# Layer 3 in column tiles, Toeplitz tiles held ahead of it, and DMAs moved between queues in a four-layer convolution kernel

## The chip, the cores and the metric

The kernel runs on one core of one Trainium2 chip. The metric is the device time of one execution in microseconds (us). A core has TensorE for matmuls (PE in the profile; its weight loads are shown apart as PEld), VectorE (DVE), ScalarE (ACT), GpSimd (POOL) and SyncE (SP). SP, ACT and POOL also issue DMAs, each in the order of its own instruction stream: an issue that has to wait holds up what stands behind it on that engine.

## The reference, cut to what matters

Four layers follow each other on `x` of shape (4, 32, 32, 16): batch, two image axes, channels.

```
_gn: group norm over 8 groups of 2 channels

# layers 0, 1, 2, each with its own M, Wp, G
inputs  = _gn(x)
first   = einsum('ijpq,bpqc->bijc', M2, inputs)
shifted = conv3x3(inputs, K(G))                 # one 3x3 filter bank for every (i, j)
diff    = relu(inputs[:, :, :, None, None, :] - shifted)
second  = einsum('ijpq,bpqijc->bijc', W2, diff)
x = x + first - second

# layer 3
inputs = _gn(x)
a, b = pad(denumerator), pad(numerators[0])
h    = irfft2(rfft2(b, (32, 32)) / rfft2(a, (32, 32)))     # a 32 x 32 filter per channel pair
y    = linear 2-D convolution of inputs with h, plus h0 at lag 0, cut to 32 x 32
x = x + y
```

## The kernel before, in words

**Layers 0 to 2.** The output positions (i, j) are worked through in 128 blks of eight positions (128 columns: eight positions of 16 filters). For one blk and one batch, called a tile here, TensorE computes the convolution as three accumulated matmuls on each half of the image (L336): `ga` and `gb` hold taps of G in float32, `gn` holds the rest, split in a high and a low part. The operands `im` are eight shifted copies of the normalised image (`im..0`, `im..1`) and four copies of its parts for the last tap (`im..2`), each of 16 channels by two halves. A half is 64 of the 128 rows, so the two halves are separate row tiles of the array. VectorE then takes the minimum with zero, multiplies with W and sums, in one pass over the two PSUM banks (L344). Four such pairs of banks exist (`ps`, bufs=4).

One W tile serves two blks; six are kept. G comes in chunks of eight blks (GC = 8): `load_g` issues five DMAs on SP, `prepare_g` subtracts on POOL (L266), casts on ACT (L270) and corrects on VectorE (L273). Two chunks of `ga`, `gb` and `gn` are kept, and one of `g9`.

**Jobs.** `conv_layer` runs the first and the last chunk of a layer in two jobs each, batches 0 and 1, then 2 and 3, so that one pair of batches can be normalised while the other is still worked on. Each of the fourteen jobs between covers a chunk with all four batches. `k` is the blk within its job. After each tile `step()` advances the pending image generators by one; after each blk of the fourteen jobs `beside` is advanced by one: first `first_term` (the M product, ending with `fd`, `xf` and `xr`), then, in layer 0, `impulse_response` (the filter of layer 3), and in layer 2 the Toeplitz loads. Program order decides the order on each engine; a `yield` is a place where the rest is put off to the next call.

**Images.** `make_image` normalises two batches (`group_norm`: sums over rows on VectorE, over groups by a matmul with `avg`), writes the image and its edges to DRAM (`img<-y` on SP, `img<-e` on ACT), and reads the shifted copies back with 24 DMAs (L166), in turn on SP and ACT. The first image of layer 0 stands alone at the start; the second is made during the first job.

**Completion semaphores.** The DMAs issued by SP and ACT share eight completion semaphores in turn, so that an issue waits until the DMA eight places ahead of it in the program has landed. POOL's DMAs have eight of their own.

**Layer 3.** The filter, written to DRAM as `hd`, is read as eight Toeplitz tiles `t` of four lags each (TQ = 4), eight DMAs a tile, three tiles at a time. For each of 32 lags `dq` and four chunks `cc`, one matmul (L564) with all 128 rows and 128 columns adds `y3`, shifted by the lag, times the filter into one bank `po`. Output position rows below the lag get zeros: `y3` is padded with 31 of them.

Where layer 3 and the W loads stand in the code:

```
lhsT=y3[:, cc, 31 - dq : 31 - dq + S, :]      # 128 columns: 32 rows of the image by 4 batches
rhs=t[:, :, q * PITCH : q * PITCH + S - 8 * cc]  # 512, 384, 256, 128 columns for cc = 0..3
...
load_g(0, 0)                                  # start: G, then one W tile, then the first image
load_w()
...
for _ in range(3):                            # after the first image: three W tiles
    load_w()
```

Of the kernel before, what the change touches and what calls it, by code (L numbers as in the profile page):

```python
# [48 lines left out]
HLEN = 8 + S * PITCH  # L49
TQ = 4  # L50


@with_exitstack
def conv_stack_kernel(ctx, tc, x, M, W, G, den, num, h0, cst, dft, one, idp, idq, out):
# [18 lines left out]
    def small_psum():  # L73
        return pair_psum()[:, 0, :]
# [20 lines left out]
    td = dram.tile([NK, 2, S, 2 * P], F32, name="td")  # L95

    def group_norm(xt):

# [3 lines left out]
        yield  # L102
        pm = small_psum()
        nc.tensor.matmul(pm[:, :2], lhsT=avg, rhs=s, start=True, stop=True)  # L104
        mean = small.tile([P, 2], F32, tag="mean", name="mean")
        nc.vector.tensor_copy(mean, pm[:, :2])
        xc = work.tile([P, 2, NBLK], F32, tag="xc", name="xc")
# [8 lines left out]
        yield  # L116
        pv = small_psum()
        nc.tensor.matmul(pv[:, :2], lhsT=avg, rhs=ss, start=True, stop=True)
        v = small.tile([P, 2], F32, tag="v", name="v")
        nc.vector.tensor_scalar(v, pv[:, :2], 1e-5, None, ALU.add)  # L120

# [13 lines left out]
    def make_image(a, xt):  # L135
# [24 lines left out]
        ]  # L160
        jobs = [(n // 4, n % 4, 0, TAPS[n]) for n in range(8)]
        jobs += [(2, n, 1 + n % 2, 8) for n in range(4)]
        for k, slot, which, tap in jobs:
            for half, q in enumerate((nc.sync, nc.scalar)):
                at, p = 64 * half + C * slot, 4 * half + tap // 3
                q.dma_start(  # L166
                    out=ims[a][k][at : at + C]
                    .bitcast(F32)
                    .rearrange("c l b cc x -> c l (b cc x)")[:, :, :RUN],
                    in_=img[a][which, p : p + 4, :, tap % 3 : tap % 3 + RUN].rearrange(  # L170
                        "l c x -> c l x"
                    ),
                )

# [5 lines left out]
    def first_term(layer, xt):  # L180
# [38 lines left out]
        for h in range(2):  # L219
            for b in range(B):  # L220
                for cc in range(2):
                    at = 64 * h + C * b
                    nc.scalar.dma_start(out=fv[h, cc, b], in_=ft[at : at + C, cc])  # L223
            yield
        xf = work.tile([P, B, NBLK], F32, tag="xf", name="xf")
        nc.scalar.dma_start(
            out=xf.rearrange("p b n -> p (b n)"), in_=fd.rearrange("p b h cc q -> p (b h cc q)")
# [10 lines left out]

    def load_g(layer, ch):
        layer, ch = at = chunk(layer, ch)  # L240
        if layer == 3 or at in gr:
            return
        ga = gs.tile([P, GC, P], F32, tag="ga", name="ga")
        gb = gs.tile([P, GC, P], F32, tag="gb", name="gb")
        g9 = gp.tile([P, GC, P], F32, tag="g9", name="g9")
        src = G[layer][:, bass.ts(ch, GC * P)]
        for half in range(2):
            rows = slice(64 * half, 64 * half + 64)
            nc.sync.dma_start(out=ga[rows].rearrange("r n m -> r (n m)"), in_=src[:64])
            nc.sync.dma_start(out=gb[rows].rearrange("r n m -> r (n m)"), in_=src[64:P])  # L250
        nc.sync.dma_start(
            out=g9.rearrange("r n m -> r (n m)"),
            in_=src[P : P + C].unsqueeze(0).to_broadcast([8, C, GC * P]),
        )
        gr[at] = ga, gb, g9
# [21 lines left out]

    def load_w():

        layer, at = divmod(len(wts), NBLK // 2)  # L280
        if layer == 3:
# [3 lines left out]
        src = W[layer][cc, :, q : q + 2, :].rearrange("p k m -> p (k m)")  # L285
        nc.sync.dma_start(
            out=wt.rearrange("p k m -> p (k m)"),
            in_=src.unsqueeze(1).to_broadcast([8, C, 2 * S * S]),
        )
        wts.append(wt)  # L290

    todo = []
# [8 lines left out]
    def conv_layer(layer, xt, finish, side=()):  # L301
# [14 lines left out]
        for job, (blks, batches) in enumerate(jobs):  # L316
            pairs = job < 2, job >= len(jobs) - 2
            for k, blk in enumerate(blks):
                if any(pairs):

                    if k in ((4, 6) if job != len(jobs) - 2 else (0, 2)):
                        load_w()
                elif k % 2 == 0:
                    load_w()
                if job:
                    if k == 1:
                        load_g(layer, blk // GC + 1)
                    if k == 6:
                        prepare_g(layer, blk // GC + 1)
                wt = wts[64 * layer + blk // 2][:, blk % 2, :]  # L330
# [34 lines left out]
    def impulse_response():  # L365
# [81 lines left out]
        with tc.tile_pool(name="fs2", bufs=1) as fs:  # L447
# [10 lines left out]
            for u in range(4):  # L458
                g = 32 * u
                nc.scalar.dma_start(out=v[g : g + 1], in_=rows[u, 0:1])  # L460
                nc.scalar.dma_start(out=v[g + 1 : g + 2], in_=rows[u, 32:33])
                nc.scalar.dma_start(out=v[g + 2 : g + 32], in_=rows[u, 2:32])
            yield
            yield
            yield
            for part in range(4):
# [15 lines left out]
            nc.gpsimd.tensor_tensor(hs[:, :, :, 0], hs[:, :, :, 0], h0s, ALU.add)  # L482
            nc.scalar.dma_start(
                out=hd[:, :8].rearrange("(n m) r -> n m r", m=4), in_=hs[:, 0, :4, S:]
            )
            for h in range(2):
                for l in range(2):
                    n = 64 * (2 * h + l)
                    nc.scalar.dma_start(
                        out=hd[n : n + 64, 8:].rearrange("m (q r) -> q m r", r=PITCH),  # L490
# [4 lines left out]
    def load_toeplitz(k):  # L495

        t = tp.tile([P, C, TQ * PITCH], F32, tag="t", name="t")
        hv = hd.rearrange("(j i) t -> i j t", j=C)
        for p in range(8):
            at = 8 + k * TQ * PITCH - p  # L500
            (nc.sync, nc.scalar)[p % 2].dma_start(
                out=t[p * C : (p + 1) * C], in_=hv[:, :, at : at + TQ * PITCH]
            )
        return t

    load_g(0, 0)
    load_w()
    images = [make_image(a, xs) for a in range(2)]
# [4 lines left out]
    drain()  # L513
    for _ in range(3):
        load_w()
    todo.append(images[1])
# [16 lines left out]

    tp = ctx.enter_context(tc.tile_pool(name="tp", bufs=3))
    ts = []

    def toeplitz():
        for k in range(3):
            ts.append(load_toeplitz(k))
            yield  # L540

    xs = conv_layer(2, xs, norm3, toeplitz())
    drain()

    xr = work.tile([P, 4, S, B], F32, tag="xf", name="xr")
    nc.scalar.copy(xr, xs.rearrange("p b (cc q) -> p cc q b", q=S))
# [7 lines left out]

    po = small_psum()
    pov = po.rearrange("n (j r) -> n j r", j=C)
    for k in range(S // TQ):
        if k and k + 2 < S // TQ:
            ts.append(load_toeplitz(k + 2))
        t = ts[k]  # L560
        for q in range(TQ):
            dq = k * TQ + q
            for cc in range(4):
                nc.tensor.matmul(  # L564
                    pov[:, :, 8 * cc :],
                    lhsT=y3[:, cc, 31 - dq : 31 - dq + S, :].rearrange("p q b -> p (q b)"),
                    rhs=t[:, :, q * PITCH : q * PITCH + S - 8 * cc],
                    start=(dq == 0 and cc == 0),
                    stop=(dq == S - 1 and cc == 3),
                )  # L570
    nc.vector.tensor_tensor(xo, xo, pov.rearrange("n j r -> n r j"), ALU.add)  # L571
    nc.sync.dma_start(out=out, in_=xo)
# [83 lines left out]
```

## Time and profile before

| | us |
|---|---|
| Time, median of 3 runs | 3216.81 (3214.71 to 3222.22) |
| The profiled execution: its time | 3216.64 |
| The profiled execution: span from first to last instruction | 3214.8 |
| Mean granted TensorE clock | 0.994 |

| engine | busy us | share of the span |
|---|---|---|
| PE | 3148.2 | 98% |
| PEld | 1678.7 | 52% |
| DVE | 2054.8 | 64% |
| ACT | 75.7 | 2% |
| POOL | 171.9 | 5% |

How to read it. The chain of waits follows the work that ended last back from the end: each piece has its start, its length and what it was, so a DMA in it is one that somebody waited for. The timeline lists instructions in order of time; a bracket at the end of a line holds how long the engine was idle before it and who released it. Groups of instructions have count, busy time, mean duration in ns and the idle time before them. Time by stretches gives the busy time of each engine between two moments, then the granted clock, the busy share of the 16 DMA engines (overlapping packets can take it above 1) and GB/s. A float32 matmul appears as two records, and so does its weight load. Names are written without the buffer numbers: `img<-y` is the DMA that writes the image to DRAM, `w<-in_W_dram` a W tile.

### The profile page before, as it was taken

Reading aid. Unit: us, or ns where it says so; the run is one execution under the profiler, and the core shown is the slowest. Engines: PE = TensorE matmul, PEld = TensorE weight load, DVE = VectorE, ACT = ScalarE, POOL = GpSimd, SP = SyncE. Lnnn points to the kernel's source line nnn. Section 1 sums busy time; section 2 is a strip of 40 time slices with the busy share of each in tenths; the row PEclk is TensorE's granted clock in tenths of the full one; section 3 lists DMA queues with packets and bytes.
Section 4 is the critical chain, followed back from the end, with each engine's and each line's share of the span. In section 5 each row is a group of like instructions: output and inputs, shape, how many; then the busy total and the mean of one; then the engine's idle time right before and its main releaser. Section 6 shows DMA issues by size and latency. Waiting matters only on the chain.

```text
span 3214.8 us, 38408 instructions
## 1 busy us (share of the span) xinstructions
PE 3148.2 (98%) x15852; PEld 1678.7 (52%) x15852; DVE 2054.8 (64%) x3294; ACT 75.7 (2%) x98; POOL 171.9 (5%) x124
## 2 busy tenths in 40 slices
PE   6999999999999999999999999999989999999998
PEld 3545566666666544444544445454444444444445
DVE  4666765666666766666666666766656666666660
ACT  0000000000000000000000000000000000000000
POOL 0002310000000000000000000000000000000000
PEclk9999999999999999999999999999999999999999
DMA  6544344343333554333433343365473343333306
GB/s 148 156 115 116 88 109 94 86 103 88 88 98 90 107 154 118 99 89 88 99 96 86 86 105 87 80 143 144 99 127 89 98 99 89 87 99 92 86 1 85
DMA packets 106383, 322.18 MB, mean 100 GB/s; under 512 B 29214, under 2 KB 59360, under 8 KB 81632
## 3 DMA queue, kind: packets, MB, share of 16 engines
q1 hardware_dynamic: 68608, 302.69, 39.2%
q10 hardware_dynamic: 37600, 17.04, 3.4%
q8 instruction: 124, 2.03, 0.3%
q14 instruction: 51, 0.42, 0.1%
HBM read 313.01 MB, written 6.68 MB: 99 GB/s over the span
## 4 chain that ended last, share of the span: by engine, by line
PE 94%; DMA 4%; DVE 1%; ACTq 0%; issue 0%; SPq 0%; POOL 0%; ACT 0%; DVEq 0%; POOLq 0%
PE pt L336 90%; PE pt L564 2%; DMA t<-hd 1%; DMA img<-y 1%; DMA im<-img 1%; PE pt L199 1%; DMA td<-s 1%; DMA v<-td 0%; DMA fd<-ft 0%; DVE junk L344 0%; DMA h0s<-in_h_dram 0%; PE pt L470 0%; ACTq L223 0%; PE pt L387 0%; POOL hs L452 0%
## 5 line engine op out<-in xcount | busy, mean ns | idle before, releaser
L344 DVE SCALAR_TENSOR_TENSOR junk<-pt,w 128x1024 f32<-128x1024 f32 x1536 | 1880.8, 1224 | 1031.7 <-PE pt L336 1017.4
L336 PE MATMUL pt<-im,ga 64*128 64x512 f32 x6144 | 1834.4, 592 | 38.0 <-DMA im<-img 20.5
L336 PE MATMUL pt<-im,gb 64*128 64x512 f32 x6144 | 1824.4, 589 | 0.9 <-DMA im<-img 0.9
L336 PE MATMUL pt<-im,gn 64*128 64x512 f32 x3072 | 1487.7, 807 | 1.9 <-DMA im<-img 1.9
L336 PEld LDWEIGHTS pt<-im,gb 64*128 64x128 f32 x6144 | 706.5, 186 | 737.7 <-issue 705.0
L336 PEld LDWEIGHTS pt<-im,ga 64*128 64x128 f32 x6144 | 708.6, 188 | 422.8 <-DVE junk L344 246.6
L336 PEld LDWEIGHTS pt<-im,gn 64*128 64x128 f32 x3072 | 355.3, 186 | 295.4 <-issue 290.2
L266 POOL TENSOR_TENSOR ga<-ga,cs 128x1024 f32<-128x1024 f32 x48 | 113.4, 2362 | 2215.5 <-DMA ga<-in_G_dram 2153.5
L273 DVE TENSOR_TENSOR gn<-g,gn 32x1024 fp32r<-32x1024 f32 x96 | 118.0, 1229 | 34.3 <-ACT gn L270 32.3
L344 DVE DVE_READ_ACCUMULATOR junk<-pt,w 128x1 f32 x1536 | 127.3, 83 | 0.0
L270 ACT CAST gn<-g 128x1024 fp32r<-128x1024 f32 x48 | 50.2, 1047 | 2318.7 <-DMA g<-in_G_dram 2020.4
L564 PE MATMUL pt<-t,y 128*128 128x512 f32 (+3 forms) x256 | 70.4, 438 | 0.0
L564 PEld LDWEIGHTS pt<-t,y 128*128 128x128 f32 x256 | 44.2, 193 | 26.2 <-issue 16.2
L571 DVE TENSOR_TENSOR xo<-xo,pt 128x512 f32<-128x512 f32 x1 | 0.7, 689 | 70.8 <-PE pt L564 70.8
L199 PE MATMUL pt<-mt,yt 128*64 128x512 f32 x96 | 21.9, 598 | 0.0
L231 POOL TENSOR_TENSOR xr<-x,xf 128x512 f32<-128x512 f32 x3 | 3.8, 1271 | 294.5 <-DMA xf<-fd 294.5
L470 PE MATMUL pt<-v,inv 64*128 64x512 f32 x16 | 8.6, 656 | 7.5 <-DMA v<-td 7.5
L199 PEld LDWEIGHTS pt<-mt,yt 128*64 128x64 f32 x96 | 6.4, 136 | 13.7 <-issue 9.4
L147 POOL COPY e<-y 32x612 f32<-32x612 f32 x6 | 4.2, 693 | 171.7 <-DVE y L146 171.7
L104 PE MATMUL pt<-s,cs 128*128 128x2 f32 x16 | 3.3, 276 | 9.7 <-DVE s L101 9.7
L408 POOL TENSOR_TENSOR H<-H,d 128x256 f32<-128x256 f32 (+1 forms) x10 | 8.2, 825 | 66.6 <-DVE d L413 66.3
L408 POOL TENSOR_TENSOR t<-s 128x256 f32<-128x256 f32 (+1 forms) x15 | 11.3, 754 | 0.0
(57 smaller groups left out, 141.0 us busy)
## 6 DMA issues: line engine op xcount, KB each, us to landing
w<-in_W_dram SPq DMA_DIRECT2D x192, 1024.0 KB
ga<-in_G_dram SPq DMA_DIRECT2D x96, 256.0 KB
gb<-in_G_dram SPq DMA_DIRECT2D x96, 256.0 KB
g<-in_G_dram SPq DMA_DIRECT2D x48, 512.0 KB
mt<-in_M_dram SPq DMA_DIRECT2D x24, 512.0 KB
t<-hd SPq DMA_DIRECT2D x32, 160.0 KB
t<-hd ACTq DMA_DIRECT2D x32, 160.0 KB
im<-img ACTq DMA_DIRECT2D x72, 67.5 KB
```

Of the source, the lines that this page charges most:

```text
L104: nc.tensor.matmul(pm[:, :2], lhsT=avg, rhs=s, start=True, stop=True)
L147: nc.gpsimd.tensor_copy(ye[a][96:, :, :, 1:, :], ys[a][96:, :, :, :3, :])
L199: nc.tensor.matmul(pf[64 * h : 64 * h + 64], lhsT=yt[:, 4 * part + k].rearrange("k b c -> k (b c)"), rhs=mts[k][:, h, :], start=(k == 0), ...
L231: nc.gpsimd.tensor_tensor(xr, xt, xf, ALU.add)
L266: nc.gpsimd.tensor_tensor(gv, gv, mid.unsqueeze(1).to_broadcast([P, GC * 8, C]), ALU.subtract)
L270: nc.scalar.copy(gn, g9)
L273: nc.vector.tensor_tensor(lo, g9[r : r + 32], lo.bitcast(F32), ALU.subtract)
L336: nc.tensor.matmul(pt[:, half, :], lhsT=w[rows, blk % GC, :], rhs=im[rows, :, b % 2, :, :S], start=n == 0, stop=n == 2,)
L344: nc.vector.scalar_tensor_tensor(junk, pt.rearrange("p h m -> p (h m)"), 0.0, wt, ALU.min, ALU.mult, accum_out=acc[b // 2][:, b % 2, blk : ...
L408: mul = lambda o, u, w: nc.gpsimd.tensor_tensor(o, u, w, ALU.mult)
L470: nc.tensor.matmul(pq[:, h, :], lhsT=inv[two], rhs=v[two, bass.ts(part, 8)].rearrange("g p m -> g (p m)"), start=True, stop=True,)
L564: nc.tensor.matmul(pov[:, :, 8 * cc :], lhsT=y3[:, cc, 31 - dq : 31 - dq + S, :].rearrange("p q b -> p (q b)"), rhs=t[:, :, q * PITCH : q ...
```

## The change

1. *Layer 3.* Of the eight Toeplitz tiles, k = 1 and k = 0 (lags 0 to 7) are done as before, with 128 columns. For lags of 8 and more some of the 32 output rows see only padding. The output rows are four blocks of eight rows (32 columns each), and from lag 8 on only the blocks are computed that can be other than zero, each as a matmul of 32 columns in one of four column tiles (partitions 32·tile of the result). A slot is four such matmuls, one in each tile, with different lags q or blocks. There are three slots for k = 3 and 2, two for k = 5 and 4, and one for k = 7 and 6, each for four `cc`. A block computed in another tile than its own goes to a bank of its own, and VectorE adds it into `xo` between the slots.
2. *Toeplitz tiles.* Five are held (TB = 5), in the order 1, 7, 6, 5, 4; their 40 DMAs are issued one in two blks during layer 2. The last three (3, 2, 0) are loaded during layer 3.
3. *Image loads.* The 24 DMAs go in turn to SP, ACT and POOL, and those that need the edges come last.
4. *W.* At the start no W tile is loaded ahead of the first image. Behind it come W 0 in two halves, W 1 and W 2; the fourth at k = 3 of the first job.
5. *G.* In the first chunk `gb` is loaded on ACT's queue. The second chunk of each layer is loaded at k = 3 of the first job, not at k = 1 of the second.
6. *POOL's queue.* `fd`, `xf`, the `v` loads and the `hd` stores are issued by POOL, not by ACT. The `v` matmuls come three blks later. `xf` shares the buffer of `ft`.
7. *Group sums.* Each is two matmuls on 64 rows instead of one on 128, added on VectorE.

The core of the diff:

```diff
+    def group_sums(s):
+        pt = pair_psum()
+        for h in range(2):
+            rows = slice(64 * h, 64 * h + 64)
+            nc.tensor.matmul(pt[:, h, :2], lhsT=avg[rows], rhs=s[rows], start=True, stop=True)
+        return pt
...
-        pm = small_psum()
-        nc.tensor.matmul(pm[:, :2], lhsT=avg, rhs=s, start=True, stop=True)
+        pm = group_sums(s)
...
-        nc.vector.tensor_copy(mean, pm[:, :2])
+        nc.vector.tensor_copy(mean, pm[:, 0, :2])
+        nc.vector.tensor_tensor(mean, mean, pm[:, 1, :2], ALU.add)
...
-        for k, slot, which, tap in jobs:
-            for half, q in enumerate((nc.sync, nc.scalar)):
-                at, p = 64 * half + C * slot, 4 * half + tap // 3
-                q.dma_start(
...
+        jobs = [(half, *tap) for tap in taps for half in range(2)]
+        jobs.sort(key=lambda job: job[4] // 3 == 2 * job[0])
+        for n, (half, k, slot, which, tap) in enumerate(jobs):
+            at, p = 64 * half + C * slot, 4 * half + tap // 3
+            (nc.sync, nc.scalar, nc.gpsimd)[n % 3].dma_start(
...
-                    nc.scalar.dma_start(out=fv[h, cc, b], in_=ft[at : at + C, cc])
+                    nc.gpsimd.dma_start(out=fv[h, cc, b], in_=ft[at : at + C, cc])
...
-        xf = work.tile([P, B, NBLK], F32, tag="xf", name="xf")
-        nc.scalar.dma_start(
+        xf = work.tile([P, B, NBLK], F32, tag="ft", name="xf")
+        nc.gpsimd.dma_start(
...
-            nc.sync.dma_start(out=gb[rows].rearrange("r n m -> r (n m)"), in_=src[64:P])
+            (other or nc.sync).dma_start(out=gb[rows].rearrange("r n m -> r (n m)"), in_=src[64:P])
...
+        n = 2 * S * S // parts
+        for k in range(parts):
+            nc.sync.dma_start(
+                out=wt.rearrange("p k m -> p (k m)")[:, bass.ts(k, n)],
+                in_=src[:, bass.ts(k, n)].unsqueeze(1).to_broadcast([8, C, n]),
+            )
+            yield
...
-                if job:
-                    if k == 1:
-                        load_g(layer, blk // GC + 1)
-                    if k == 6:
-                        prepare_g(layer, blk // GC + 1)
+                if len(wts) == 3 and k == 3:
+                    list(load_w())
+                if k == (3 if job == 0 else 1):
+                    load_g(layer, blk // GC + 1)
+                if job and k == 6:
+                    prepare_g(layer, blk // GC + 1)
...
-                nc.scalar.dma_start(out=v[g + 2 : g + 32], in_=rows[u, 2:32])
-            yield
-            yield
-            yield
+                nc.gpsimd.dma_start(out=v[g + 2 : g + 32], in_=rows[u, 2:32])
+            for _ in range(6):
+                yield
...
-                    nc.scalar.dma_start(
+                    nc.gpsimd.dma_start(
                         out=hd[n : n + 64, 8:].rearrange("m (q r) -> q m r", r=PITCH),
...
-    load_g(0, 0)
-    load_w()
+    load_g(0, 0, nc.scalar)
...
-    for _ in range(3):
-        load_w()
+    for parts in (2, 1, 1):
+        list(load_w(parts))
...
+    order = [1, 7, 6, 5, 4, 3, 2, 0]
     def toeplitz():
-        for k in range(3):
-            ts.append(load_toeplitz(k))
-            yield
+        for k in order[:TB]:
+            for _ in load_toeplitz(k):
+                yield
+                yield
...
+    slots = [
+        [[(None, None, q)] for q in range(TQ)],
+        [[(0, i + 1, 3)] + [(t, t, i) for t in range(1, 4)] for i in range(3)],
+        [[(0, 2, 2 + i), (1, 3, 2 + i), (2, 2, i), (3, 3, i)] for i in range(2)],
+        [[(t, 3, t) for t in range(4)]],
+    ]
...
+    for n, k in enumerate(order):
+        if n and n + TB - 1 < len(order):
+            list(load_toeplitz(order[n + TB - 1]))
+        for slot in slots[k // 2]:
+            for cc in range(4):
+                for tile, block, q in slot:
+                    at = 31 - TQ * k - q
+                    if tile is None:
+                        bank, cols, width = po, slice(0, P), S
+                    else:
+                        bank = po if tile == block else other[block]
+                        cols, width = slice(32 * tile, 32 * tile + 32), 8
+                        at += 8 * block
+                    nc.tensor.matmul(
+                        bank[cols].rearrange("n (j r) -> n j r", j=C)[:, :, 8 * cc :],
+                        lhsT=y3[:, cc, at : at + width, :].rearrange("p q b -> p (q b)"),
+                        rhs=ts[n][:, :, q * PITCH : q * PITCH + S - 8 * cc],
...
+        if k == 6:
+            add(3, 2, other[3])
+        elif k == 4:
+            add(3, 1, other[3])
+        elif k == 2:
+            for block in range(1, 4):
+                add(block, 0, other[block])
```

## Prediction

> **What bounds the kernel now.** I read the page's totals first, then the chain of waits in order of time, then the timeline at each place where the chain leaves the matmuls, and last the busy time by stretches there.
>
> ```profile
> PE 3148.2 (98%) x15852; PEld 1678.7 (52%) x15852; DVE 2054.8 (64%) x3294; ACT 75.7 (2%) x98; POOL 171.9 (5%) x124
> 10.96 12.46 DMA img<-y
> 24.33 3.32 DMA im<-img
> 27.67 3.27 DMA im<-img
> 30.96 3.28 DMA im<-img
> ...
> 46.44 14.34 DMA img<-y
> ...
> 101.56 4.39 issue
> ...
> 247.15 3.58 PE pt L199 x16
> ...
> 490.19 9.15 PE pt L336 x37
> ...
> 500.88 7.18 PE pt L336 x37
> ...
> 3140.71 70.21 PE pt L564 x256
> ```
>
> TensorE is busy 98% of the span, and nearly all of it is L336, which the change does not shorten. What can move is outside it: 34.9 us before the first complete tile, four holes, and the 70.2 us of layer 3. The holes, from the timeline, with their idle time in brackets:
>
> ```profile
> 105.95 2.08 PE L336 MATMUL pt<-im,ga 64*128 64x512 f32 x4 [4.39 <-issue]
> 488.15 1.19 PE L470 MATMUL pt<-v,inv 64*128 64x512 f32 x1 [7.48 <-DMA v<-td]
> 2367.91 2.08 PE L336 MATMUL pt<-im,ga 64*128 64x512 f32 x4 [13.05 <-DVE junk L344]
> 2363.06 1.04 ACT L270 CAST gn<-g 128x1024 fp32r<-128x1024 f32 x1 [120.56 <-DMA t<-hd]
> 519.41 27.85 ACTq L489 DMA_DIRECT2D hd<-hs  x4
> ```
>
> The first waits for G of chunk 1, the second for `v`, the third for `gn`, which sat on ACT behind 12 Toeplitz loads. The fourth hole is 1.1 us at 71 (second image). A hole also cools the clock: after 105.95 the first two tiles end 2.3 and 0.9 us late against the steady 1.963 us per tile, so 3.2 us per hole; after 488 the granted clock was 0.50 and 0.59.
>
> Time by stretches (columns: PE, PEld, DVE, ACT, POOL, then clock, DMA share, GB/s):
>
> ```profile
> 14.00:22.00 8.00, 0.00 (x0) 0.00 (x0) 2.86 (x3) 0.39 (x1) 0.16 (x1) 1.00 0.49 117
> 24.00:34.00 10.00, 4.45 (x8) 1.50 (x8) 0.00 (x0) 0.00 (x0) 0.00 (x0) 1.00 0.90 172
> 34.00:60.00 26.00, 25.23 (x117) 12.79 (x116) 16.85 (x35) 1.31 (x3) 0.69 (x1) 1.00 0.53 140
> 3152.00:3196.00 44.00, 44.00 (x165) 27.88 (x165) 0.00 (x0) 0.00 (x0) 0.00 (x0) 1.00 1.20 143
> ```
>
> At 14 to 22 only one W tile and `img<-y` are on the way: half the DMA share, about 1 MB in 8.5 us. So a W tile takes 8.5 us and fills half of the engines; `img<-y`, issued at 10.96, had to pass it (undisturbed, in layer 1, it takes about 3 us). The same at 34 to 60: three W tiles (25.5 us), then `img<-y` at 60.8.
>
> A tile below is one blk of one batch: its matmuls, then one VectorE pass with W.
>
> **The start.** *First image.* W leaves the queue ahead of `img<-y`; G stays, with `gb` on ACT. Its two issues (0.6 us each) delay ACT's table load to about 4, and the square root behind it is due at 8.35: nothing. G was in at 13.35 (ACT's `gn` starts), so the image is in DRAM at about 14.3, not 23.4. Then 24 loads of 67.5 KB. SP and ACT share eight completion semaphores, so eight are under way, in three rounds of 3.3 us; POOL brings eight of its own. Rounds alone say 6.6 us. The Trainium skill, "DMA: Bandwidth & Descriptors", Rules for kernel authors, says that spreading DMAs over SP, ACT and GpSimd doesn't help bandwidth, since all run on the same 16 engines: then 10.8 us stay. The stretch 24 to 34 is 0.90 busy at 172 GB/s, close to the rule: I take 9 us. First tile about 24 instead of 34.9.
>
> *W behind it.* W tile n serves blks 2n and 2n+1, and four are needed by the first two jobs. W 0 to 2 now start at about 23 (W 0 in two halves, the first in at 28 for a VectorE pass due at 26, which four PSUM buffers cover) and end at 23.4+25.5 = 49; the second `img<-y` sits behind them on SP and lands at 50 (before: 60.8). Its loads take to 59. The fourth W tile (blks 6, 7) is issued at k=3, thus behind those loads on SP: issued at 58, landed at about 68. VectorE then holds tiles 12 to 15 of the first job, all four PSUM buffers, until 68. TensorE, done with them at 59, idles to 69.2: a new hole of 10 us, where none was. Job 1 then ends at 69.2+3.2+16x1.963 = 103.8. Before, job 2 began at 105.95 and paid 3.2: 109.15. G of chunk 1 is issued right behind W 3, in by 77, and prepared at k=6: the old hole is gone. Gain **5.3** us, of 10.9 that the first tile gains. Bounds: 1 (a W tile later still) to 18 (W 3 in time).
>
> **v, and what moves to POOL.** The `v` matmuls go three blks later: 3x7.85 = 23.5 us. `v` was 7.5 late, so 16 us are spare for POOL's 12 loads, which no longer queue on ACT behind `h0s` (8 us). Gain 7.5+3.2 = **10.7**. The price of a POOL DMA is in no row. Low: ACT's rows (0.9 us per large `v`, 0.44 per `fd`, 27.85 for the four `hd`). High: three times that. I take ACT's, since the transfers of `hd` themselves need such a time. Behind it on POOL stands L266's `ga` (2.4), without which the next chunk can't start. `fd`: 16 DMAs, `xf`, `xr` begin at k=0, 55 us before the chunk ends; on ACT 24 us in layer 0; 2 us each still fit. `hd`: issued after the last ACT copy, by my count at 533 in the old clock, next job at 570: 34 us less than 27.85 plus setup leaves 5. That is thin, and the first rival. Image loads on POOL, layers 1 and 2: eight by 1 us, ahead of a job boundary with 8 us to spare: nothing.
>
> **The Toeplitz stall.** 40 pieces, one in two blks (15.7 us), instead of 24 at once; ACT's `gn` has at most two pieces ahead of it per chunk, and `fd` and `xf` are off ACT. Gain 13.05+3.2 = **16.2**. Their 6.5 MB, spread over ten chunks of 63 us, add 10 GB/s to the 100 of the page, and SP, which issues half of them ahead of its W and G, has time: it waits for VectorE to free a W buffer 1732 us in all. `xf` in the buffer of `ft` adds a wait that has a whole layer.
>
> **Layer 3.** Now 32 lags x four cc, each 512 to 128 columns: 2.13 us per lag of pure stream (70.2 less a cold start). After: eight lags stay whole (k=1 and 0): 9.8 with the cold start, and 8.5. The other 24 become 12 slots of four column tiles. Do four run at once, and do their weights come in time? Three groups bear on it (the last is of the chain):
>
> ```profile
> L199 PE MATMUL pt<-mt,yt 128*64 128x512 f32 x96 | 21.9, 598 | 0.0
> L564 PEld LDWEIGHTS pt<-t,y 128*128 128x128 f32 x256 | 44.2, 193 | 26.2 <-issue 16.2
> ...
> 290.20 0.87 PE pt L387 x8
> ```
>
> L199 has two column tiles of 64: a float32 matmul is two records, 427 ns of pace for 512 columns in L564, and 16 of them are through in 3.58 us, half of what one after another would need. So two tiles do run side by side. The Trainium skill's "TensorE: Matmul & The Clock Gate", The mechanism, says that a weight load passes a running matmul only if its row group differs; here all four tiles share all rows. By that rule the eight loads of a step, about 110 ns each (my estimate from 136 at 64 columns and 190 at 128), would be exposed, 42 us over 48 steps, and layer 3 would take 86. But L564 itself has 44.2 us of weight loads under 70.2 us of matmuls in one row group, hidden: the row decides. What remains is the issue rate: 8 load-and-matmul pairs per step, whose stream is 853, 640, 427, 213 ns. Nearest row: L387, 8 pairs in 0.86 us, itself limited by stream, so an upper bound: 41 us for 48 steps. The page (Back-to-back issue gap) gives about 81 ns per pair at 128 columns: 650 per step, 2.8 us per slot, 33.6 in all, my estimate; stream alone 25.6. Sum 9.8+33.6+8.5 = 51.9, gain **18.3** (10 to 24). Loads: five tiles took 3150.5 to 3198, 9.4 us each; three now, from 9.8 on, the last at 38 or 39, needed at 43: covered, by 4 us only, and late by 3 or 4 if slots run at 2.13. VectorE's small additions between the slots (a full one takes 0.69) run under the 8.5 us of k=0; the last addition stays.
>
> **Group sums.** Each becomes two matmuls on half of the rows, which run side by side as L336's halves do, and one more VectorE addition (0.17 with its gap 0.2). In the layers TensorE has other tiles meanwhile (it idles 0.37 there now). After the last tile both sums are on the path: two additions cost 0.4, the halves may save 0.1: -0.3.
>
> **Sum.** 5.3+10.7+16.2+18.3-0.3 = 50.2. From the profiled 3216.64 (span 3214.8 and 1.84 around it): 3166.4; the median of the runs is 0.17 higher: **3167**.
>
> **Rivals.**
> - *POOL is late with `hd`, and still faster.* Each `hd` DMA is 2048 pieces of 160 B. At 12 us each the four need 48, `ga` comes 15 late, 18 with the cold clock: 3185. For: software writes these descriptors (same DMA page, SWDGE vs HWDGE), and no row prices them; against: ACT's own rows, held by the transfer.
> - *The same, slower than before.* It decides from about 20 us per `hd` DMA: four are 80, `ga` 47 late, 3.2 cold, and the gain is gone. At 25 us each: 66+3 lost, 3236.
> - *Column tiles one after another*: 12x4x2.13 = 102 instead of 33.6: 3236. L199 speaks against.
> - *Pairs cost L387's 107 ns*: 41 instead of 33.6: 3175.
> - *W 3 in time*: 3154. That would need SP to issue it before the second image's loads; its place in the queue speaks against.
>
> **Chances.** Forecast 0.60; `hd` late but faster 0.17; pairs dear 0.09; W 3 in time 0.04; `hd` so late that it is slower 0.05; tiles serial 0.03; all of it cancelling 0.02. Faster 0.90, same 0.02, slower 0.08, with 0.2% (6 us) as what a measurement of this kernel can tell. Range 3147 (layer 3 at stream rate, W in time) to 3198 (`hd` 30 late).
>
> **What would show it.** First complete tile near 24; second `img<-y` near 50; PE idle some 10 us before 69, its releaser VectorE's tile, that in turn waiting for W; no hole at 102, 481 or 2355; the layer 3 line near 52 us; no idle PE behind POOL's `ga` at about 540 to 560. It is wrong if W 3 lands before 59, if `ga` follows `hd` late, or if a step of four column tiles takes 0.9 us at 128 columns as at 512.

## The result, and the profile after

| | before | after |
|---|---|---|
| Time, median of 4 runs, us | 3217.98 (3214.71 to 3222.22) | 3174.86 (3173.18 to 3175.76) |
| The profiled execution: its time, us | 3216.64 | 3174.82 |
| Its span, us | 3214.8 | 3173.0 |

The ratio is 0.9865, with a 95% interval from 0.9848 to 0.9882. The forecast was 3167; the profiled execution gained 41.8 us, not 50.2. Three of the four large terms came out within 1.1 us of the forecast, that of layer 3 by two errors that cancel; the first, the start, had the wrong sign.

First the chain of waits of the kernel after, at the start and in layer 3 (start, length, what it was):

```profile
14.39 2.84 DMA im<-img
...
23.06 12.04 DMA w<-in_W_dram
...
39.42 15.46 DMA img<-y
...
61.64 17.40 DMA w<-in_W_dram
...
3117.51 10.67 PE pt L606 x32
3129.61 9.59 DMA t<-hd
3139.21 11.02 DMA t<-hd
3150.26 9.56 DMA t<-hd
3160.06 8.88 PE pt L606 x32
```

The reader is to see two things. W 3, issued at 61.64 behind the second image's loads, took 17.4 us, so the second job began at 80.45. And layer 3 is now held by three Toeplitz loads, one after the other: 10.67 of matmuls, 30.2 of loads, 8.88 of matmuls.

The timeline shows the start's hole, on VectorE and then on TensorE (idle time in brackets), and the first complete tile:

```profile
24.85 2.17 PE L351 MATMUL pt<-im,ga 64*128 64x512 f32 x4 [16.83 <-DMA im<-img]
79.17 1.23 DVE L359 SCALAR_TENSOR_TENSOR junk<-pt,w 128x1024 f32<-128x1024 f32 x1 [20.10 <-DMA w<-in_W_dram]
80.45 2.15 PE L351 MATMUL pt<-im,ga 64*128 64x512 f32 x4 [17.21 <-DVE junk L359]
```

To book the gain by stage I take pieces of the chain that both kernels have and subtract their starts: the transposes of `first_term` behind the second job of each layer (L186, after: L197), VectorE's sum at the end of layers 0 and 2 (`x`), and VectorE's last pass of batches 0 and 1 in layer 2 (at 3100.31, after: 3077.01). Before and then after:

```profile
124.79 0.59 PE pt L186 x4
...
1053.62 0.44 DVE x L359
...
1165.11 0.59 PE pt L186 x4
...
2181.60 0.59 PE pt L186 x4
...
3100.31 1.25 DVE junk L344 x2
...
3134.49 0.44 DVE x L359
```

```profile
129.41 0.59 PE pt L197 x4
...
1046.80 0.44 DVE x L374
...
1157.58 0.59 PE pt L197 x4
...
2173.36 0.59 PE pt L197 x4
...
3077.01 1.24 DVE junk L359 x2
...
3110.83 0.44 DVE x L374
```

The start lost 4.6 us. At the end of layer 0 the kernel after is 6.8 ahead, so the step from -4.6 is worth 11.4 and holds the `v` stage. At the transposes of layers 1 and 2 it is 7.5 and 8.2 ahead. In layer 2 it comes to 23.3 ahead, a step of 15.1 that holds the Toeplitz stall, and at the layer's end to 23.7. Layer 3 itself takes 51.4 instead of 70.2. TensorE has no idle entry between 470 and 600, behind `v` and `hd`, nor where the Toeplitz stall was.

### The profile page after: what moved, and what is told of

Its sections match the earlier page's. It is cut to its first block, busy times and chain, and to the rows that moved or that the text cites. A ratio compares the mean times of both kernels' runs of the same rounds, so it can differ in the third digit from the quotient of the medians.

```text
span 3173.0 us, 38930 instructions
## 1 busy us (share of the span) xinstructions
PE 3111.1 (98%) x16076; PEld 1720.0 (54%) x16076; DVE 2060.4 (65%) x3315; ACT 75.9 (2%) x98; POOL 235.6 (7%) x240
## 4 chain that ended last, share of the span: by engine, by line
PE 96%; DMA 3%; DVE 1%; issue 0%; ACT 0%; SPq 0%; ACTq 0%; DVEq 0%
PE pt L351 94%; DMA t<-hd 1%; DMA w<-in_W_dram 1%; PE pt L210 1%; PE pt L606 1%; DMA img<-y 0%; DMA im<-img 0%; DMA g<-in_G_dram 0%; DVE junk L359 0%; PE pt L402 0%; PE pt L445 0%; PE pt L103 0%; PE pt L484 0%; DVE x L374 0%; DVE s L110 0%
## 5 line engine op out<-in xcount | busy, mean ns | idle before, releaser
L351 PE MATMUL pt<-im,ga 64*128 64x512 f32 x6144 | 1681.2, 591 | 36.7 <-DVE junk L359 19.9
L351 PE MATMUL pt<-im,gb 64*128 64x512 f32 x6144 | 1673.0, 588 | 0.0
L351 PE MATMUL pt<-im,gn 64*128 64x512 f32 x3072 | 1347.3, 806 | 0.0
L351 PEld LDWEIGHTS pt<-im,gb 64*128 64x128 f32 x6144 | 693.2, 185 | 647.6 <-issue 571.9
L351 PEld LDWEIGHTS pt<-im,ga 64*128 64x128 f32 x6144 | 681.0, 187 | 410.9 <-DVE junk L359 249.7
L281 ACT CAST gn<-g 128x1024 fp32r<-128x1024 f32 x48 | 50.2, 1047 | 2322.7 <-DMA g<-in_G_dram 1894.2
L606 PE MATMUL pt<-t,y 128*32 128x512 f32 (+4 forms) x448 | 46.2, 439 | 5.4 <-DMA t<-hd 4.6
L234 POOL DMA_DIRECT2D fd<-ft x48 | 25.1, 532 | 223.5 <-DVE ft L227 213.2
L606 PEld LDWEIGHTS pt<-t,y 128*32 128x32 f32 (+1 forms) x448 | 24.9, 124 | 26.7 <-issue 18.0
L177 POOL DMA_DIRECT2D im<-img x48 | 24.5, 518 | 27.0 <-DMA img<-y 20.5
```

What stands on the lines that cost most here:

```text
L177: (nc.sync, nc.scalar, nc.gpsimd)[n % 3].dma_start(out=ims[a][k][at : at + C] .bitcast(F32) .rearrange("c l b cc x -> c l (b cc x)")[:, :, ...
L234: nc.gpsimd.dma_start(out=fv[h, cc, b], in_=ft[at : at + C, cc])
L281: nc.scalar.copy(gn, g9)
L351: nc.tensor.matmul(pt[:, half, :], lhsT=w[rows, blk % GC, :], rhs=im[rows, :, b % 2, :, :S], start=n == 0, stop=n == 2,)
L606: nc.tensor.matmul(bank[cols].rearrange("n (j r) -> n j r", j=C)[:, :, 8 * cc :], lhsT=y3[:, cc, at : at + width, :].rearrange("p q b -> p ...
```

## The experiments

Every run was timed beside the kernel before; its median in the groups of runs was 3214.3 to 3218.0. A ratio's interval is about 0.0015 to each side, 5 us, which is as large as most of the effects. So the ratio says roughly how large an effect is, and the trace says where it is. All are edits of the kernel after (ratio 0.9865); the last two combine several.

| run | median us | ratio to before | 95% interval |
|---|---|---|---|
| G one blk later | 3177.24 | 0.9882 | 0.9867 to 0.9897 |
| W 3 early | 3168.68 | 0.9854 | 0.9839 to 0.9869 |
| W 0 to 3 early, in eight DMAs each | 3169.01 | 0.9855 | 0.9840 to 0.9870 |
| layer 3 in descending order | 3170.66 | 0.9861 | 0.9845 to 0.9878 |
| v on POOL, three blks | 3179.75 | 0.9888 | 0.9872 to 0.9904 |
| v on ACT, six blks | 3174.55 | 0.9870 | 0.9856 to 0.9883 |
| G behind W 6 | 3187.90 | 0.9910 | 0.9897 to 0.9923 |
| W 3 between write and loads, loads on two queues | 3186.95 | 0.9902 | 0.9886 to 0.9918 |
| image loads on SP and ACT | 3171.80 | 0.9867 | 0.9851 to 0.9884 |
| layer 3 in whole lags | 3195.78 | 0.9939 | 0.9927 to 0.9952 |
| W 3 early, and layer 3 | 3164.11 | 0.9844 | 0.9830 to 0.9857 |
| W 3 between, and layer 3 | 3162.36 | 0.9842 | 0.9829 to 0.9856 |

**What holds W 3?** G of chunk 1 was the first suspect, since its issues follow W 3's within 0.8 us.

```diff
-                if k == (3 if job == 0 else 1):
+                if k == (4 if job == 0 else 1):
                     load_g(layer, blk // GC + 1)
```

> Only the place of one issue differs from the kernel after: the G loads of chunk 1 are issued one blk later, at k=4, so that W 4 and not G stands behind W 3 on SP's queue. Theory 1 (W 3 shared the DMA engines with G, issued 0.8 us behind it): W 3 lands about 8.5 to 9.5 us after its issue at 61.6, as W 1 and W 2 did one after another, so at about 71; the second job's first tile starts near 72.4 instead of 80.45, and the time is about 8 us under the kernel after: 3167. Rival 2 (W 3 was held by the image loads ahead of it on the engines, and G behind it is harmless): W 3 lands at 79 as now, 3175. Rival 3 (whatever stands behind a transfer on the queue takes part of its engines, W 4 as well as G): 79 or later too, and then W 4's own landing is near W 3's.

From the timelines of this run, SP's issue and VectorE's wait:

```profile
63.23 1.68 SPq L300 DMA_DIRECT2D w<-in_W_dram  x2
65.67 0.51 SPq L260 DMA_DIRECT2D ga<-in_G_dram  x1
81.76 1.23 DVE L359 SCALAR_TENSOR_TENSOR junk<-pt,w 128x1024 f32<-128x1024 f32 x1 [21.58 <-DMA w<-in_W_dram]
```

W 3 took 18.5 us, no less than before, so theory 1 as I put it fell. But G was only 2.4 us behind W 3, and so not away. The next edit keeps it away for good, in layer 0 alone:

```diff
-                if k == (3 if job == 0 else 1):
+                if (k == 4 if layer == 0 and job < 2 else k == (1 if job else 3)) and (job or layer):
                     load_g(layer, blk // GC + 1)
```

> From the kernel after, with one edit in layer 0: the G loads of chunk 1 are issued in the second job behind W 6, whose buffer comes free only when that job has done its first two blks, so that no G is under way while W 3 is; W 4 and W 5 follow W 3 at once. In the run with G one blk later W 3 landed 18 us after its issue, as in the kernel after, with G 4 us behind it. Theory 1 (G, wherever it stands behind W 3, takes part of a limit that all loads share): W 3 lands 9 to 12 us after its issue at 61.6, at 71 to 74, the hole at 80 shrinks by 5 to 8 us; G then lands near 95 and the old hole at the second job's end is back with 0 to 5 us: 3167 to 3175. Rival 2 (the image loads ahead of W 3 hold it) and rival 3 (W 4 and W 5 behind it share with it just as G does): W 3 lands at 79 as now, and the time is 3175 plus the hole of G, 3175 to 3183; with rival 3, W 4 lands within a few us of W 3.

```profile
62.03 28.84 SPq L300 DMA_DIRECT2D w<-in_W_dram  x4
76.65 1.23 DVE L359 SCALAR_TENSOR_TENSOR junk<-pt,w 128x1024 f32<-128x1024 f32 x1 [18.02 <-DMA w<-in_W_dram]
125.37 2.08 PE L351 MATMUL pt<-im,ga 64*128 64x512 f32 x4 [12.83 <-issue]
```

With no G on the way W 3 still landed at 76.6, 14.6 us after its issue. G is therefore worth some 2 to 3 us of the delay and not 8. The packets of this run show where the rest is. From 62 to 66, 497 of 505 packets were smaller than the 8 KB pieces in which W is read: the image loads ahead of W 3. From 66 to 76 hardly anything but W was on the way, about one tile of it. In the kernel after, 129 of the 217 packets in that stretch were smaller, G's among them (first this run, then the kernel after, both from 66 to 76):

```profile
DMA packets 145, 1.09 MB, mean 109 GB/s; under 512 B 11, under 2 KB 12, under 8 KB 12
```

```profile
DMA packets 217, 1.12 MB, mean 112 GB/s; under 512 B 31, under 2 KB 31, under 8 KB 129
```

So the image loads ahead of W 3 held it (rival 2), and G took a part. W 4 and W 5, issued right behind W 3 (rival 3), can have had little: the 1.09 MB are hardly more than W 3's own. Keeping G away also has its price: SP issued G only at 90.9, and the hole that the change had removed was back with 12.83 us, more than the 0 to 5 I had allowed.

**W 3 ahead of the image.**

```diff
-    for parts in (2, 1, 1):
+    for parts in (2, 1, 1, 1):
         list(load_w(parts))
```

> W 3 is issued with W 0 to 2, ahead of the second image's write, instead of at k=3 behind the image loads. All theories: no VectorE pass waits for W from 59 on. What is late next is the second image: its write stands behind four W tiles instead of three, so it lands near 64 instead of 54.9 if the queue serves in order, its loads near 71, and the second job starts near 71.5 instead of 80.45: 9 us faster than the kernel after, 3166. If the queue does not serve in order, the write lands near 56, the loads near 64, W 3 near 66, and it is 3158.

VectorE's passes at the end of its waits for W 2 and W 3, SP's issue of the second image's loads, and TensorE's first tile with them:

```profile
53.42 1.23 DVE L359 SCALAR_TENSOR_TENSOR junk<-pt,w 128x1024 f32<-128x1024 f32 x1 [3.87 <-DMA w<-in_W_dram]
62.52 1.22 DVE L359 SCALAR_TENSOR_TENSOR junk<-pt,w 128x1024 f32<-128x1024 f32 x1 [3.85 <-DMA w<-in_W_dram]
63.65 6.16 SPq L177 DMA_DIRECT2D im<-img  x8
73.59 2.17 PE L351 MATMUL pt<-im,ga 64*128 64x512 f32 x4 [10.77 <-DMA im<-img]
```

W 3 came 9.1 us behind W 2 with the image's write issued behind it, and the write landed 1 us later, at 63.65: on SP's queue it did not pass the W tiles. (That is not a strict order of bytes: above, G's packets moved while W 3, ahead of it on the same queue, was still on the way.) The second job started 6.9 us earlier than at 80.45, where I had expected 9. The image loads took 9.9 from the write's landing to the first tile.

**W in more pieces.** W 0 to 3 early, each tile in eight DMAs:

```diff
+            for p in range(8):
+                nc.sync.dma_start(
+                    out=wt.rearrange("p k m -> p (k m)")[p * C : (p + 1) * C],
+                    in_=src[p : p + 1].to_broadcast([C, 2 * S * S]),
+                )
```

> As the run before it, with W 0 to 3 early, but each of these four tiles is loaded by eight DMAs of 16 partitions (one row of W copied to 16 partitions each) instead of one of 8 rows by 16 copies. Theory A (one such DMA keeps only half of the engines busy, the share was 0.5 while W alone was under way): a tile takes about 4.5 us instead of 8.5 to 9.3, SP's 32 issues of 0.6 us set the pace (22 to 41), the second image's write lands near 45, its loads near 52, no hole at 80 is left and the second job starts at about 57 and ends near 89 instead of 115: about 26 us faster than the kernel after, 3149. Rival B (120 GB/s is what these reads give, however many engines): a tile still takes 8.5, as the run before: 3166. Rival C (the many issues delay SP's queue: the image write is issued at 41 and its loads later than ACT's): a few us of it lost, 3153.

The stretch from 26 to 32 us (PE, PEld, DVE, ACT, POOL, then clock, DMA share, GB/s), of the run with W 3 early in single DMAs, and then of this one, with SP's issues below it:

```profile
26.00:32.00 6.00, 6.00 (x25) 3.71 (x24) 1.06 (x1) 0.00 (x0) 0.00 (x0) 1.00 0.51 124
```

```profile
26.00:32.00 6.00, 6.00 (x24) 3.63 (x22) 0.00 (x0) 0.00 (x0) 0.00 (x0) 1.00 1.06 138
21.98 32.97 SPq L300 DMA_DIRECT2D w<-in_W_dram  x32
SPq L300 <- DMA img<-e: 6.8, 1, 6.8
```

The share of the engines doubled and the rate rose from 124 to 138 GB/s only, 7.6 us for a tile of 1 MB instead of 8.5: rival B. Half a share did not mean that half of the rate was free. Rival C came true as well: SP was busy with the 32 issues until 54.95. One of them waited 6.8 us for ACT's edge write to land (the last line: what SP waited for, total us, times, longest), since both share the completion semaphores; from 42 to 48 the rate was down to 33 to 75 GB/s, and the image's write was issued at 55.68 instead of 39.37. What the pieces would gain without that wait no run shows.

**W 3 between the image's write and its loads.** Twice: first with the loads on ACT and POOL only, as in the diff, then without the lines on `queues`, that is with the three queues of the kernel after.

```diff
         nc.scalar.dma_start(out=edge(9), in_=flat(ye[a][:C]))
+        queues = nc.sync, nc.scalar, nc.gpsimd
+        if len(wts) == 3:
+            list(load_w())
+            queues = nc.scalar, nc.gpsimd
         yield
```

> From the kernel after: W 3 is issued on SP right behind the second image's write (at 40, instead of 61.6), and the 24 loads of that image go to ACT and POOL only, so that none stands behind W 3. Theory (queues serve in order; start bound by the bytes to be moved): the image's write lands at 55 as now, behind W 2; its loads take until 63 to 65 beside W 3; W 3, which they share the engines with, lands near 66 to 68 instead of 79; VectorE then frees the buffers and the second job starts near 68 instead of 80.45: 12 us faster than the kernel after, 3163. Rival (image loads and W together slow down as W 3 and G did): W 3 at 72 or later and the second job at 73, no better than with W 3 ahead of the image's write: 3168.

The first three lines are of the chain of waits, the others of the timelines:

```profile
40.32 32.74 DMA ga<-in_G_dram
73.08 13.54 DMA g<-in_G_dram
86.99 11.94 DMA im<-img
55.12 32.32 ACTq L181 DMA_DIRECT2D im<-img  x12
70.88 1.23 DVE L363 SCALAR_TENSOR_TENSOR junk<-pt,w 128x1024 f32<-128x1024 f32 x1 [11.60 <-DMA w<-in_W_dram]
91.05 2.30 PE L355 MATMUL pt<-im,ga 64*128 64x512 f32 x4 [27.61 <-DMA im<-img]
```

W 3 did come 8 us earlier, but the image loads took 36 us. My edit had moved one thing more than I saw: with no image load on SP, nothing kept SP from issuing G of chunk 1, its first piece already at 40.32, and so G was on the way ahead of the image. The chain shows what that cost: `g`, G's last piece, was issued when the first had landed, and one of ACT's image loads, which shares the completion semaphores with SP, only when `g` had landed, at 86.6. The second run keeps SP's eight loads ahead of G. It also has the edits of layer 3 below.

> As the run with the three edits together, but W 3 is issued on SP between the second image's write and its loads, which keep their three queues: the eight loads on SP stand behind W 3 and ahead of G. Theory (one queue serves in order, two queues share): the write lands at 55, W 3 at 66, the image loads at about 70, the second job starts there instead of at 73.6: 3 to 4 us faster than W 3 ahead of the write, 3159. Rival (small image loads crawl beside W's large packets, as when W 3 stood there and ACT and POOL had all 24 loads, with G beside them too): the second job starts at 76 or later, 3165 or more.

```profile
64.56 1.23 DVE L361 SCALAR_TENSOR_TENSOR junk<-pt,w 128x1024 f32<-128x1024 f32 x1 [7.96 <-DMA w<-in_W_dram]
70.04 2.17 PE L353 MATMUL pt<-im,ga 64*128 64x512 f32 x4 [9.27 <-DMA im<-img]
```

The second job starts at 70.04, as expected, 10.4 us earlier than in the kernel after. W 3 is no longer what it waits for.

**Two queues or three for the image.**

```diff
-            (nc.sync, nc.scalar, nc.gpsimd)[n % 3].dma_start(
+            (nc.sync, nc.scalar)[n % 2].dma_start(
```

> From the kernel after, with one edit: the 24 image loads go to SP and ACT only, in turn, as in the kernel before (their new order stays). Theory 1 (the rule: spreading over a third queue brings no bandwidth): the first image's loads take 10.5 to 10.8 from 14.4 on, the first tile starts at 24.9 to 25.2 as now, the second image's are the same, W 3 lands at 79: 3175. Rival 2 (eight more loads under way at once shorten it): the loads take 12 to 13.5, the first tile starts at 27 or later, W 3 lands at 81 or later: 3177 to 3179.

```profile
20.00:22.00 2.00, 0.00 (x0) 0.00 (x0) 0.00 (x0) 0.00 (x0) 0.00 (x0) 1.00 1.02 177
23.18 2.21 PE L351 MATMUL pt<-im,ga 64*128 64x512 f32 x4 [15.27 <-DMA im<-img]
```

The same stretch in the kernel after:

```profile
20.00:22.00 2.00, 0.00 (x0) 0.00 (x0) 0.00 (x0) 0.00 (x0) 0.00 (x0) 1.00 1.13 127
```

The first tile starts at 23.18, earlier than in any run with three queues (24.5 to 26.5): 8.8 us behind the first load instead of 10.5. The third queue did not help, and seems to cost a little: from 20 to 22, with only image loads on the way in both, the rate was 127 GB/s with three queues and 177 with two. A part of the 1.7 us may be W 0, which SP, with eight loads instead of twelve, issued at 22.02 and not 23.00, beside the last image loads. The intervals of the two ratios overlap, so the time does not settle it.

**v: the queue or the three blks?** The first run undoes the blks, the second the queue.

```diff
-            for _ in range(6):
+            for _ in range(3):
                 yield
```

```diff
-                nc.gpsimd.dma_start(out=v[g : g + 1], in_=rows[u, 0:1])
+                nc.scalar.dma_start(out=v[g : g + 1], in_=rows[u, 0:1])
...
```

> From the kernel after, with one edit: the generator yields three times between the loads of v and its matmuls, as in the kernel before, not six; the loads stay on POOL. Theory (the later blks did it, POOL alone did not): POOL has issued the last v load 17 us after inv's load, and v lands up to 12 us behind an issue, so it is in 28 to 29 us after inv where three blks leave 23.2; TensorE waits about 5 us and pays 3 for the cold clock: 8 us slower than the kernel after, 3183. Rival (POOL did it, by not standing behind h0s): no hole, 3175.

> From the kernel after, with one edit: the twelve loads of v go back to ACT's queue; the six yields stay. Theory (the later blks did it): v lands 30.7 us after inv's load as in the kernel before, six blks leave 46.7, no hole: 3175, the same as the kernel after. Rival (the queue did it): the hole of 7.5 us and the cold clock are back, 3185.

The first run's timeline:

```profile
492.38 1.19 PE L484 MATMUL pt<-v,inv 64*128 64x512 f32 x1 [4.72 <-DMA v<-td]
```

TensorE waited 4.72 us for `v` (5 expected), and the clock behind it was 0.68 of full speed from 490 to 500. The median rose by 4.9 rather than 8, with runs from 3174.9 to 3185.5. The second run has no idle entry there, and its time is that of the kernel after. So the three blks do it; POOL's queue, with three blks, saves some of the 7.5 us but is not needed.

**Layer 3.** First the column tiles are undone: every lag is whole again, the five held tiles and their order stay.

```diff
-    slots = [
-        [[(None, None, q)] for q in range(TQ)],
-        [[(0, i + 1, 3)] + [(t, t, i) for t in range(1, 4)] for i in range(3)],
-        [[(0, 2, 2 + i), (1, 3, 2 + i), (2, 2, i), (3, 3, i)] for i in range(2)],
-        [[(t, 3, t) for t in range(4)]],
-    ]
+    slots = [[[(None, None, q)] for q in range(TQ)]] * 4
```

> From the kernel after, with one part undone: in layer 3 every lag is one matmul over all 128 columns again, 32 lags by four cc; the five held tiles and their order stay, and VectorE has only the last addition. Theory (the column tiles alone shorten layer 3, the held tiles only make the loads keep up): 2.13 us per lag and the cold start, 70.2 us as in the kernel before, three loads of 10 us hidden: 18.8 us slower than the kernel after, 3193.7. Rival (a part of the gain is from having five tiles ahead): less than 70.

The chain of waits of this run:

```profile
3118.65 71.19 PE pt L601 x256
```

71.2 us, like the kernel before: without the column tiles the gain of layer 3 is gone, and the held tiles alone give nothing. What the column tiles would give with three tiles held no run shows. Next, the order:

```diff
-    order = [1, 7, 6, 5, 4, 3, 2, 0]
+    order = [7, 6, 5, 4, 3, 2, 1, 0]
...
+    first = [[(t, t, 0) for t in range(4)]]
+    of = lambda k: first + slots[0][1:] if k == 1 else slots[k // 2]
```

> Only layer 3 differs from the kernel after: the Toeplitz tiles are held and used in the order 7, 6, 5, 4, 3, 2, 1, 0 instead of 1, 7, 6, 5, 4, 3, 2, 0, so that the first buffer comes free after one slot instead of four full lags, and the full lags stand last; the first full lag is done as four column tiles. Theory L (three loads of 10 us, one after the other and behind the first tile, set the end of layer 3; a slot runs at the stream's 2.13 to 2.3 us): loads land about 14, 24 and 34 after its start, work of 22, 29, 37 and 45.6 is always behind them, so layer 3 takes about 45.5 instead of 51.4: 3169. Rival P (slots cost 2.8 us by the issue of 8 pairs per step, and the idle time in the trace is only the end of the loads): 2+33.6+17 = 52.6, no change, 3175 to 3176.

The chain:

```profile
3117.17 5.47 PE pt L608 x64
3123.44 21.79 PE pt L608 x320
3145.98 17.68 PE pt L608 x88
```

No load is left in the chain. Layer 3 took 46.5 us (45.5 expected by theory L, 52.6 by rival P). Ten slots took 21.79 us, 2.18 each: 2% over the stream's 2.13, not my 2.8. Two waits of 0.8 us were for VectorE's additions.

**Together.** W 3 early, the descending order, and the additions of block 3 put off:

```diff
-        if k == 6:
-            add(3, 2, other[3])
-        elif k == 4:
+        if k == 4:
+            add(3, 2, other[3])
             add(3, 1, other[3])
```

> From the kernel after, two edits that had gained alone, together: W 3 issued with W 0 to 2 (3168.7 alone), and layer 3 in the order 7 to 0 (3170.7 alone); and a third, for the two waits of 0.8 us of TensorE for VectorE's additions in that order: both additions of block 3's tiles 1 and 2 come after k=4, and the accumulators of the other blocks lie in PSUM tiles of their own, apart from that of the whole lags. Theory (the parts are on the path one after another and add): 3174.9 - 6.2 - 4.2 - 1.7 = 3162.8, layer 3 at about 44.8 us and no wait for the additions in it. Rival (the additions or the loads hold it elsewhere): layer 3 stays at 46.5, 3164.5.

3164.1 (3160.9 to 3165.2). The second job started at 73.4. The two waits for VectorE were gone, yet layer 3 took 47.9 and not 44.8: the cold clock lasted longer (0.50 and then 0.68 in its first 6 us, where the run before had 0.65 and 1.00), and TensorE idled 1.1 ahead of k = 1, for which the profile names no cause. With W 3 between write and loads instead it is 3162.4 (3160.6 to 3166.5), the lowest median of all. None of its runs reaches those of the kernel after, 3173.2 to 3175.8; the intervals of the two ratios just overlap. That both combinations are faster rests on the traces: at the second job 7.1 and 10.4 us earlier, and in layer 3 3.5 and 4.2 shorter.

## Why the prediction was right, and where it failed

In the profiled executions the gain was 41.8 us of the 50.2 forecast: right in kind and within the range, short by the start.

| step | expected gain | in the traces |
|---|---|---|
| start | 5.3 | -4.6 |
| v and POOL | 10.7 | 11.4 |
| Toeplitz stall | 16.2 | 15.1 |
| layer 3 | 18.3 | 18.8 |
| group sums | -0.3 | 1.3 |

The remaining -0.2 is the store of the result.

- *The start is the step that failed.* It had W 3 issued at 58 and landed at 68, 10 us later; it was issued at 61.6 and landed at 79.1, 17.4 us later. The issue was 3.6 late because the second image's write landed at 54.9 and not 50: of the three W tiles ahead of it, W 0, beside the end of the first image's loads, took 12.0 us, and W 1 and W 2 9.3 each, where I had 8.5. Of the 7.4 us by which W 3 itself took longer, G behind it is 2.9 (14.5 us in the run without G). Of the other 4.5, 3 are the image loads ahead of it: by the packets of that run they were in at about 66, 4 us behind W 3's issue, where I had 1; and 1.5 is W 3 itself, 10.5 us from there instead of 9. I had taken each transfer's time from a stretch where it was nearly alone and added nothing for neighbours. That W 3 set the second job's start is shown by moving it: the job then began 6.9 and 10.4 us earlier. What the prediction had right is the place and the kind of the new hole, and that the old hole at 102 is gone.
- *The image loads.* The Trainium skill's "DMA: Bandwidth & Descriptors", Rules for kernel authors, says that a third issuing engine brings no bandwidth. I had gone some two fifths of the way from the rule's 10.8 towards the rounds' 6.6; the kernel after took 10.5, and 8.8 with two queues. The runs agree with the rule, and the count of rounds was not what set the time.
- *v* went as worked out, and both single edits fit: 4.7 us late with three blks, nothing with six on either queue. *`hd` on POOL*, the first rival and the mechanism of the slower one, did not happen. POOL's queue (timeline of the kernel after):

```profile
536.68 4.22 POOL L503 DMA_DIRECT2D hd<-hs  x4 [25.46 <-issue]
540.91 2.37 POOL L277 TENSOR_TENSOR ga<-ga,cs 128x1024 f32<-128x1024 f32 x1
```

  I had bounded it by ACT's 27.85 from below, since the transfers themselves seemed to need that time. They did not. These are the packets of ACT's queue before (519 to 547) and of POOL's after (530 to 560): count, MB, share of the engines.

```profile
q10 hardware_dynamic: 6047, 0.93, 25.6%
q0 software_dynamic: 384, 1.31, 32.3%
```

  On ACT's queue a packet was about as small as one piece of 160 B; on POOL's it held 3.4 KB on average, and the four landed 5.0 to 9.6 us after their issue.
- *The Toeplitz stall* went, and nothing took its place. That the pieces come one in two blks and that `fd` and `xf` left ACT were changed together; no run separates the two.
- *Group sums* had the wrong sign. Behind the last tile they cost 0.5 us, near the 0.3 worked out. But for each of the five pairs of batches that are normalised while TensorE has other tiles they seem to gain 0.36: 0.7 at the turn to layer 1, 0.7 at the turn to layer 2, 0.4 before the last pair. In these stretches TensorE has no idle entry but the 0.4 us ahead of the first group sum in both kernels, and on it only the group sums differ. No run undoes them alone.
- *Layer 3* came out at 51.4 where I had 51.9, by two errors that cancel. Slots at 2.8 us were too dear: 32 load-and-matmul pairs in 2.18 us are 68 ns a pair on average, where the page "TensorE: Matmul & The Clock Gate", Back-to-back issue gap, had led me to 81. The step of 128 columns shows it best: the other three steps of a slot need 1.92 us for their stream alone, which leaves 0.26 us for its eight pairs, 33 ns each at most. The loads then were not covered: the last landed 42.3 after the start of layer 3 and not 38 or 39, since the first buffer came free at 10.7 and three loads took 30.2. I had named this case (late by 3 or 4 at 2.13 a slot) and not taken it. The rule of that page's The mechanism, that a weight load passes a matmul only if its row group differs, gave 86 us; four column tiles over all rows ran at stream pace. (The same section also lets a load pass that goes to a background weight buffer, which I had left out.)

## What to carry to other kernels

Cost a transfer by what is on the way with it, not by its time alone: at a start that is all transfers, as here, the late ones ended about where the bytes ahead of them did, and an issue that is moved behind another image's loads moves its landing by those loads. When a stage of matmuls is made shorter, ask again whether the loads beside it still fit; here the order of use, cheapest tile first, brought back what they cost. Before taking an issue off a queue, see what that issue kept from running ahead: without image loads on SP, G overtook the image.

## What the runs showed of the hardware that I had not expected

- The four `hd` DMAs (2048 pieces of 160 B each) held POOL's queue for 4.22 us, against 27.85 on ACT, and went in packets of 3.4 KB on average instead of about 160 B; an image load took 0.52 us to issue on POOL.
- A W tile read in eight DMAs instead of one put the share of busy DMA engines at 1.06 instead of 0.51, with 138 GB/s instead of 124.
- With 24 image loads on two queues the first tile started 8.8 us behind the first load, with three 10.5.
- G, issued behind a W tile on the same queue, moved its packets while that tile was still on the way, and the tile took 17.4 us instead of 14.5.
- Four column tiles with a weight load for each matmul ran at 2.18 us per slot, 2% over the stream's 2.13; at 128 columns that is at most 33 ns for a load and its matmul.
